# Where VectorE's spare steps stand between two seeds of a key-tile pair, in a four-layer graph network on one Trainium2 core

## The chip, the cores and the metric

The kernel runs on one core of one Trainium2 chip. Every time here is in device microseconds (us) of that core, for one launch. A core has five engines with a queue each: TensorE (PE, matrix products into PSUM banks), VectorE (DVE), ScalarE (ACT, here the exponentials), GpSimd (POOL) and SyncE (SP, which issues most DMAs). An engine takes its queue strictly in program order and waits at an instruction until the semaphores that it names are there; whatever stands behind it in that queue waits too.

## The reference

Four layers over a graph of N = 3327 nodes with 128 features, each `x = x + layer(relu(layernorm(x)), adj)`. Almost all of the time lies in the first, a graph attention with the adjacency added twice as a bias. It makes 128 heads (`d`) with 8 numbers each:

```python
q = (x @ Wq.T).reshape(d, n, h)            # d = 128 heads, n = 3327 nodes, h = 8
k = (x @ Wk.T).reshape(d, n, h)
v = (x @ Wv.T).reshape(d, n, h)
a = jnp.einsum('dnh,dmh->dnm', q, k) * scale
a = a + spatial_encoding + edge_encoding    # both are adj here
a = jax.nn.softmax(a, axis=2)
out = jnp.einsum('dnm,dmh->dnh', a, v)
return out.reshape(n, h * d) @ Wo.T
```

The other three (hyperbolic graph layers and a two-way message layer) are products with `adj` or its transpose and stand after the attention.

## The kernel before

**The attention's loops.** The scores are made transposed: key tiles of 128 rows on the partitions, queries along the free axis. The 3327 queries are cut into 7 *chunks* of 476 (index `c`), the 128 heads into 32 *groups* of four (`g`), the 26 key tiles into 13 *pairs* (`q`, 0 to 12; `r` is 0 or 1 inside the pair). So there are 7 x 32 x 13 = 2912 pairs `u`, 224 groups, and in each pair four heads `j`.

**What happens to one pair.** A pair holds two of seven PSUM banks. VectorE *seeds* each bank with adjacency minus a row bound (`seed(u, r)`, L641). TensorE adds the scores of head 0 (`scores(u, 0)`, L650), ScalarE takes the exponential of both banks at once (`exps`, L662 for 952 columns, L665 where the banks do not lie side by side and each is done alone), then TensorE adds the difference to head 1 in the same bank (the query operand holds head j minus head j-1), and so on to head 3. After the exponential of head 3 the bank is free for a later pair: `seed(m+1, 1)` and `seed(m+2, 0)` both follow the exponential of `(m-2, 3)`. The exponentials are multiplied with V into one bank `po` (`values`, L705), which VectorE copies out once a group (`store`, L713).

**The order is written out by hand.** One loop runs `i` over slots, four to a pair. In slot `i` ScalarE gets one exponential; `at = i % 4` says which of the pair's slots it is. I write `q4@0` for the slot with `at == 0` of pair 4 of a group. ScalarE's order is: `@0` head 0 of pair m, `@1` head 3 of m-2, `@2` head 2 of m-1, `@3` head 1 of m. VectorE's seeds come at `@1` (`seed(m+1, 1)`) and `@2` (`seed(m+2, 0)`). The slot in which something is written down gives its place in the queue of its engine, nothing else.

**Exponentials by hand.** In the pairs 0, 2, 5, 7 and 10 (`BY_HAND`) the exponential of head 0 of `r = 1` is made by VectorE, so that ScalarE has only one bank to do there. `hand_exp(u)` is a generator: its first step, in `@0` of the pair, is `mul` (L683, which reads the raw scores out of the bank) and the seed of that bank; then come the steps k3, k2, k1 (L687) and fin (L689, times `EA`), one for each `next()`. TensorE needs the result four pairs later. `EA` is the exponential of the bias alone, made for each chunk by `bare(c, q)`: a subtraction on VectorE (L674) and an exponential on ScalarE (L675), the second waiting for the first. For the chunks after the first, `bare` is written down eight pairs ahead, so in the pairs 5, 7, 10 and 12 of a chunk's last group and pair 2 of the next one's first.

**Squares.** The transposed adjacency and the row maxima of the chunks to come are made on the side: a `Square` of 128 rows is loaded in four quarters (`load`: four DMAs of 104 KB by SP into the only buffer `rows`), each quarter is turned in two halves (`turn`, L288, VectorE) and reduced (`largest`, L292, VectorE). Then come `gather`, `back`, `finish` and `store` (a DMA of 1664 KB). `plan` puts them under the number of a pair; in `@0` of that pair they are written down (`behind`). Three or four squares belong to a chunk, one every seven groups, 22 in the loop.

**SP's queue.** At pair 1 of each group `load_qk` and `load_v` put the next group's 40 or so loads into SP's queue; at pair 4 GpSimd is given `negate_q` (L566), `spread_v` (L576) and `all_here` for them.

Of the kernel before, what the change touches and what calls it, by code (L numbers as in the profile page):

```python
# [29 lines left out]
NQ = NT // 2  # L30
# [8 lines left out]
NG = HEADS // 4  # L39
# [25 lines left out]
def rows_of(t):  # L65
    return P - 1 if t == NT - 1 else P
# [11 lines left out]
def width_of(c):  # L78

    return min(CW, N + 1 - c * CW)  # L80


def squares_of(c):

    return 0 if c < 0 else -(-min(CW * (c + 1), NP) // P)
# [3 lines left out]
def gnn_kernel(ctx: ExitStack, tc: tile.TileContext, x, adj, Wq, Wk, Wv, Wo, embed, layer,  # L89
# [174 lines left out]
    class Square:  # L264
# [29 lines left out]
        def store(self):  # L294
            nc.sync.dma_start(by_tile[:, :, self.s * P:(self.s + 1) * P].rearrange("t p n -> p t n"), self.cols)
# [30 lines left out]
    with tc.tile_pool(name="a1", bufs=1) as a1, tc.tile_pool(name="a2", bufs=2) as a2, \  # L326
# [23 lines left out]
        for t0 in range(0, NT, 2):  # L350
            for s in "kq":
# [3 lines left out]
                for i in range(2):  # L355
                    t = t0 + i
                    sq = a4.tile([P, H, P], F32, name="sq")
# [82 lines left out]
    with tc.tile_pool(name="d1", bufs=1) as d1, tc.tile_pool(name="d2", bufs=2) as d2, \  # L440
# [17 lines left out]
        with tc.If(loose > 0):  # L458
            for s in range(squares_of(0), NT):
                square(d2, s, d2)  # L460
            for t in range(NT):
                m = rows_of(t)
# [24 lines left out]
            for c in range(NC):  # L487
# [5 lines left out]
                with tc.For_i(0, HEADS, 1) as d:  # L493
# [12 lines left out]
                    for t in range(NT):  # L506
                        m = rows_of(t)
                        s = d_ps.tile([P, 4 * P], F32, name="ps_y")
# [16 lines left out]
    with tc.tile_pool(name="e1", bufs=1) as e1, tc.tile_pool(name="e_adj", bufs=28) as e_adj, \  # L525
# [69 lines left out]
        with tc.If(loose < 1), tc.manual_schedule():  # L595
# [11 lines left out]
            pairs = [(c, g, q) for c in range(NC) for g in range(NG) for q in range(NQ)]  # L607
            n = len(pairs)
            adj_of, shift_of, v_of, e_of, here = {}, {}, {}, {}, {}
            by_vector = deque()  # L610
# [13 lines left out]
            def touch(u, rows, x):  # L624
                of = {banks(u)[r] for r in rows}
                for y, other in touched:
                    if not of & other and x.ins.engine != y.ins.engine:
                        tc.declare_no_dep(x.ins, y.ins, reason="other banks")
                for i in of:
                    if i in last:  # L630
                        tc.add_manual_dep(x.ins, last[i].ins.name, after, reason="the same bank")
                    last[i] = x
                touched.append((x, of))

            def bank(u, r):
                return S[:, banks(u)[r], :width_of(pairs[u][0])]

            def seed(u, r):
                c, g, q = pairs[u]
                w = width_of(c)  # L640
                touch(u, [r], nc.vector.tensor_tensor(bank(u, r), adj_of[c][2 * q + r][:, :w], shift_of[c][:, :w],  # L641
                                                      op=ALU.subtract))

            def scores(u, j):
                c, g, q = pairs[u]
                w, b = width_of(c), (c * NG + g) % 2
                for r in range(2):
                    hand = r == 1 and by_hand(u)
                    q_s = QZ[b] if hand and j == 1 else QS[b][:, j, :]
                    x = nc.tensor.matmul(  # L650
                        bank(u, r), KT[b][64 * r:64 * r + 64, max(0, j - 1), q * P:(q + 1) * P],
                        q_s[64 * r:64 * r + 64, :w], start=hand and j == 0, stop=True, skip_group_check=True)
                    if (j, q, r) == (0, 0, 0):
                        tc.add_manual_dep(x.ins, here.pop(c * NG + g).ins.name, after, reason="the loads")
                    touch(u, [r], x)

            def exps(u, j):
                w, (even, odd) = width_of(pairs[u][0]), banks(u)
                e = e_of[u, j] = e_e.tile([P, 2, CW], F32, name=f"e{j}", bufs=(5, 4, 3, 2)[j])
                hand = j == 0 and by_hand(u)  # L660
                if even > odd and not hand:
                    touch(u, (0, 1), nc.scalar.activation(e[:, :, :w], S[:, odd:even + 1, :w], AF.Exp, scale=2.0))  # L662
                    return
                for r in range(1 if hand else 2):
                    touch(u, [r], nc.scalar.activation(e[:, 1 - r, :w], bank(u, r), AF.Exp, scale=2.0))  # L665

            def by_hand(u):

                return 0 <= u < n and pairs[u][2] in BY_HAND

            def bare(c, q):

                w = width_of(c)
                nc.vector.tensor_tensor(EA[q][:, :w], adj_of[c][2 * q + 1][:, :w], shift_of[c][:, :w], op=ALU.subtract)  # L674
                nc.scalar.activation(EA[q][:, :w], EA[q][:, :w], AF.Exp, scale=2.0)  # L675

            def hand_exp(u):


                w = width_of(pairs[u][0])  # L680
                s = e_h.tile([P, CW], F32, name="h")[:, :w]
                e = e_of[u, 0][:, 0, :w]
                touch(u, [1], nc.vector.tensor_scalar(s, bank(u, 1), EXP_ARG, None, op0=ALU.mult))  # L683
                seed(u, 1)
                yield
                for k in (3, 2, 1):
                    nc.vector.scalar_tensor_tensor(e, s if k == 3 else e, EXP_C[k], s, op0=ALU.add, op1=ALU.mult)  # L687
                    yield
                nc.vector.scalar_tensor_tensor(e, e, EXP_C[0], EA[pairs[u][2]][:, :w], op0=ALU.add, op1=ALU.mult)  # L689
# [11 lines left out]
            def values(u, r):  # L701
                c, g, q = pairs[u]
                w, k = width_of(c), c * NG + g
                for j, (v, of) in enumerate(heads_of(u, r)):
                    nc.tensor.matmul(po[32 * j:32 * j + H + 1, :w], VA[k % 2][:, 2 * pairs[v][2] + of, j, :],  # L705
                                     e_of[v, j][:, 1 - of, :w], start=(q == 0 and r == 0),
                                     stop=(q == NQ - 1 and r == 1))
# [31 lines left out]
                        adj_of[c + 1].append(load_adj(c + 1, len(adj_of[c + 1])))  # L739


            behind = {}

            def plan(u, f, *a):
                behind.setdefault(u, []).append((f, a))

            def plan_squares(c):
                for k, s in enumerate(range(squares_of(c), squares_of(c + 1))):
                    sq, u = Square(e_t, s), (c * NG + 7 * k + 1) * NQ
                    for j in range(4):  # L750
                        plan(u, sq.load, j)
                        plan(u + 4, sq.turn, j, 0)
                        plan(u + 9, sq.turn, j, 1)
                        plan(u + 12, sq.largest, j)
                        u += NQ
                    for k, f in ((0, sq.gather), (1, sq.back), (7, sq.finish), (8, sq.store)):
                        plan(u + k, f)

# [8 lines left out]
            for c in range(NC):  # L767
                for q in BY_HAND:
                    u = c * NG * NQ + q
                    if u:  # L770
                        plan(u - 8 if c else u - 1, bare, c, q)
            bare(0, 0)

            def in_slot(i):

                j = -i % 4
                return (i - 3 * j) // 4, j


            for i in range(-4, 4 * n + 15):  # L780
                u, j = in_slot(i)
                if 0 <= u < n:
                    exps(u, j)
                at = i % 4
                if i == -4:
                    seed(0, 0)
                if at == 0 and by_hand(i // 4):
                    by_vector.append(hand_exp(i // 4))
                    next(by_vector[-1])
                for k in range(0 if at % 3 else 1 if at else 0 if by_hand(i // 4) else 2):  # L790
                    if by_vector and next(by_vector[0], True):
                        by_vector.popleft()
                if at == 0 and i > 0:
                    for f, a in behind.pop(i // 4, ()):
                        f(*a)
                if at == 1 and (i + 3) // 4 < n and not by_hand((i + 3) // 4):
                    seed((i + 3) // 4, 1)
                u = (i - 14) // 4
                if at == 2 and 0 <= u < n and pairs[u][2] == NQ - 1:
                    store(u)  # L800
                if at == 2 and (i + 6) // 4 < n:
                    seed((i + 6) // 4, 0)
                if at % 2:
                    for k in (1, 2):
                        u, j = in_slot(i + k)
                        if 0 <= u < n:
                            scores(u, j)
                    u, r = ((i - 11) // 4, 0) if at == 3 else ((i - 13) // 4, 1)
                    if 0 <= u < n:
                        values(u, r)  # L810
                if at == 0 and 0 <= i // 4 < n:
                    loads(i // 4)
# [19 lines left out]
    def arr(name, w=D):  # L832
        return big.tile([P, NT, w], F32, name=name)

    xs, ys, hT, uT = arr("xs"), (arr("y0"), arr("y1")), big.tile([P, NP], F32, name="hT"), big.tile([P, NP], F32, name="uT")
    a, w1 = arr("a", D + 1), arr("w", D + 1)
# [587 lines left out]
```

## Time and profile before

| what | value |
|---|---|
| three runs: median, lowest, highest | 11043.86, 11043.25, 11045.12 us |
| the profiled execution, its span | 11043.15 us, 11041.4 us |
| first to last exponential of the attention | 451 to 10207 us |
| ScalarE busy from 500 to 10100 us | 9533.5 of 9600 us |
| TensorE, VectorE, GpSimd busy there | 9491.1, 7872.5, 1915.4 us |
| busy before it, 0 to 451 us: TensorE, VectorE, ScalarE | 188.8, 214.2, 163.6 us |
| busy behind it, 10206 to 11041.4 us | 737.1, 478.0, 212.9 us |
| granted TensorE clock, whole run | 0.983 |

A row of the profile gives the start, the length, the engine, the line, the operation, what it writes and reads, and in brackets the idle time before it and what ended that. Records of ScalarE overlap: one that starts 0.84 us after the one before lasts 0.97 us. Its busy share therefore hides short losses, and the distance from start to start is what counts.

### The profile page before, as it was taken

The numbers are of one execution on the slowest core, as the hardware profiler recorded it, in microseconds if no ns is written. First come the engines' busy times: TensorE is split into PE (matmuls) and PEld (weight loads), VectorE is DVE, ScalarE is ACT, GpSimd is POOL, SyncE is SP. The second block draws the span as 40 slices with busy tenths as digits, with TensorE's granted clock in tenths as the row PEclk, the third lists the DMA queues.
The fourth block names the chain that finished last, engine by engine and source line by source line (L and its number), as shares of the span: only waits on it lengthen the run. The fifth ranks groups of instructions, "written<-read, shape, count | busy, mean of one in ns | idle before, by whom it ended". The sixth has DMA issues, their size and how long they took to land. (4 is left out here: it accounts for less than half of the span.)

```text
span 11041.4 us, 206142 instructions
## 1 busy us (share of the span) xinstructions
PE 10565.6 (96%) x72876; PEld 3427.7 (31%) x72876; DVE 8678.3 (79%) x13452; ACT 10058.1 (91%) x13816; POOL 2173.9 (20%) x3149
## 2 busy tenths in 40 slices
PE   4599999999999999999999999999999999999889
PEld 2133322333223322233322333222222233332544
DVE  5588887888878887788887888878887787887655
ACT  3599999999999999999999999999999999999330
POOL 5121221121211221221211211211212121211101
PEclk7799999999999999999999999999999999999899
DMA  8755555555555554555545555455545544543668
GB/s 250 253 99 92 98 97 105 98 98 91 99 110 92 98 97 82 110 98 92 99 90 112 99 96 94 91 117 92 99 86 89 109 87 80 88 83 67 199 234 282
DMA packets 697364, 1257.08 MB, mean 114 GB/s; under 512 B 195218, under 2 KB 557737, under 8 KB 683279
## 3 DMA queue, kind: packets, MB, share of 16 engines
q1 hardware_dynamic: 646060, 1114.42, 50.1%
q0 software_dynamic: 50272, 129.37, 4.1%
q8 instruction: 590, 9.67, 0.4%
q14 instruction: 442, 3.62, 0.1%
HBM read 1096.53 MB, written 146.60 MB: 113 GB/s over the span
## 5 line engine op out<-in xcount | busy, mean ns | idle before, releaser
L662 ACT ACTIVATE e<-S 128x952 f32<-128x952 f32 (+1 forms) x9024 | 8316.9, 1076 | 42.3 <-PE S L650 28.4
L705 PE MATMUL po<-e,VA 128*9 128x476 f32 (+1 forms) x46592 | 5738.7, 564 | 32.5 <-DVE OS L713 16.8
L641 DVE TENSOR_TENSOR S<-a,shb 128x476 f32<-128x476 f32 (+1 forms) x5824 | 4016.1, 690 | 1330.2 <-ACT e L662 968.4
L650 PE MATMUL S<-QS,KT 64*128 64x476 f32 (+1 forms) x22176 | 4543.4, 443 | 89.4 <-DVE S L641 29.6
L650 PEld LDWEIGHTS S<-QS,KT 64*128 64x128 f32 x22176 | 2081.6, 184 | 5096.2 <-issue 1284.8
L665 ACT ACTIVATE e<-S 128x476 f32<-128x476 f32 (+1 forms) x4128 | 2418.3, 689 | 3.7 <-PE S L650 2.9
L687 DVE SCALAR_TENSOR_TENSOR e<-e,h 128x476 f32<-128x476 f32 (+1 forms) x2240 | 1550.6, 692 | 77.1
L566 POOL TENSOR_SCALAR QS<-QS 32x476 fp32r<-32x476 f32 (+1 forms) x1344 | 1092.7, 813 | 1541.4 <-DMA QS<-qS_d 986.1
L717 POOL DMA_DIRECT2D oT_d<-OS x896 | 470.6, 530 | 4538.9 <-DVE OS L713 4494.6
L705 PEld LDWEIGHTS po<-e,VA 128*9 128x9 f32 x46592 | 691.0, 88 | 1641.1 <-issue 1522.5
L683 DVE TENSOR_SCALAR h<-S 128x476 f32<-128x476 f32 (+1 forms) x1120 | 727.8, 650 | 261.6 <-PE S L650 259.6
L689 DVE SCALAR_TENSOR_TENSOR e<-e,EA 128x476 f32<-128x476 f32 (+1 forms) x1120 | 824.0, 736 | 0.0
L687 DVE SCALAR_TENSOR_TENSOR e<-h 128x476 f32<-128x476 f32 (+1 forms) x1120 | 767.7, 685 | 0.0
L1047 PE MATMUL pu<-strip,y 128*128 128x512 f32 (+2 forms) x1456 | 600.5, 567 | 45.2 <-issue 29.2
L650 PE MATMUL S<-QZ,KT 64*128 64x476 f32 (+1 forms) x1120 | 487.6, 435 | 12.6 <-DVE S L641 8.5
L576 POOL COPY VA<-VR 128x832 f32<-128x832 f32 x224 | 247.0, 1103 | 970.8 <-DMA VR<-v_d 659.8
L1047 PEld LDWEIGHTS pu<-strip,y 128*128 128x128 f32 (+1 forms) x1456 | 273.0, 192 | 322.6 <-issue 289.3
L1051 DVE TENSOR_REDUCE deg<-strip 128x1 f32<-128x1536 f32 (+3 forms) x104 | 192.8, 1881 | 74.1 <-DMA strip<-in_adj_dram 40.8
L650 PEld LDWEIGHTS S<-QZ,KT 64*128 64x128 f32 x1120 | 205.3, 183 | 113.6 <-DVE S L641 63.9
L999 ACT COPY uT<-pu 128x512 f32<-128x512 f32 (+1 forms) x21 | 11.2, 554 | 244.3 <-PE pu L1047 244.3
L288 DVE STREAM_TRANSPOSE cols<-rows 128x416 f32<-128x416 f32 x208 | 205.2, 991 | 26.3 <-DMA rows<-in_adj_dram 18.5
L713 DVE COPY OS<-po 128x476 f32<-128x476 f32 (+1 forms) x224 | 146.3, 653 | 97.5 <-PE po L705 97.5
(242 smaller groups left out, 1973.2 us busy)
## 6 DMA issues: line engine op xcount, KB each, us to landing
KT<-kS_d SPq DMA_DIRECT2D x1792, 208.0 KB
KT<-kS_d SPq DMA_DIRECT2D x1792, 104.0 KB
VR<-v_d SPq DMA_DIRECT2D x224, 416.0 KB
QS<-qS_d SPq DMA_DIRECT2D x3072, 14.9 KB
QS<-qS_d SPq DMA_DIRECT2D x1536, 29.8 KB
adjT<-cols SPq DMA_DIRECT2D x26, 1664.0 KB
a<-adjT SPq DMA_DIRECT2D x156, 238.0 KB
rows<-in_adj_dram SPq DMA_DIRECT2D x309, 104.0 KB
```

Source lines behind the costliest of these rows:

```text
L566: nc.gpsimd.tensor_scalar(QS[b][r0:r0 + 32, j + 1, :w], QS[b][r0:r0 + 32, j, :w].bitcast(F32), -1.0, 0.0, op0=ALU.mult, op1=ALU.add)
L576: nc.gpsimd.tensor_copy(VA[(c * NG + g) % 2][:, :, :, 0:H], v.rearrange("p j (t e) -> p t j e", e=H))
L641: touch(u, [r], nc.vector.tensor_tensor(bank(u, r), adj_of[c][2 * q + r][:, :w], shift_of[c][:, :w], op=ALU.subtract))
L650: x = nc.tensor.matmul(bank(u, r), KT[b][64 * r:64 * r + 64, max(0, j - 1), q * P:(q + 1) * P], q_s[64 * r:64 * r + 64, :w], start=hand an ...
L662: touch(u, (0, 1), nc.scalar.activation(e[:, :, :w], S[:, odd:even + 1, :w], AF.Exp, scale=2.0))
L665: touch(u, [r], nc.scalar.activation(e[:, 1 - r, :w], bank(u, r), AF.Exp, scale=2.0))
L683: touch(u, [1], nc.vector.tensor_scalar(s, bank(u, 1), EXP_ARG, None, op0=ALU.mult))
L687: nc.vector.scalar_tensor_tensor(e, s if k == 3 else e, EXP_C[k], s, op0=ALU.add, op1=ALU.mult)
L689: nc.vector.scalar_tensor_tensor(e, e, EXP_C[0], EA[pairs[u][2]][:, :w], op0=ALU.add, op1=ALU.mult)
L705: nc.tensor.matmul(po[32 * j:32 * j + H + 1, :w], VA[k % 2][:, 2 * pairs[v][2] + of, j, :], e_of[v, j][:, 1 - of, :w], start=(q == 0 and r ...
L717: nc.gpsimd.dma_start(oT_d[:, d * N + c * CW:d * N + c * CW + w], o[32 * j:32 * j + H + 1, :w])
L1047: nc.tensor.matmul(got[c][:, :k], y[:m, t, :], s[:m, c * 4 * P - c0:c * 4 * P - c0 + k], start=(t == 0), stop=(t == NT - 1))
```

## The change

The polynomial steps no longer stand at `@3` (one) and `@0` (two) but together behind `seed(m+2, 0)` at `@2`: three, two where `store` stands there as well, none where the next pair is one by hand. Behind them, from a second table `between`, come the turns, the row maxima and `bare`. The square's places are counted anew: its twelve operations stand at the pairs 8 and 11 of six groups, the first quarter's load at pair 2 of the first of them, each further load one pair behind the maximum that frees the buffer; the rest follows from the seventh group on.

```diff
-            behind = {}
+            behind, between = {}, {}
 
-            def plan(u, f, *a):
-                behind.setdefault(u, []).append((f, a))
+            def plan(u, f, *a, into=behind):
+                into.setdefault(u, []).append((f, a))
 
             def plan_squares(c):
                 for k, s in enumerate(range(squares_of(c), squares_of(c + 1))):
-                    sq, u = Square(e_t, s), (c * NG + 7 * k + 1) * NQ
+                    sq, u = Square(e_t, s), (c * NG + 7 * k) * NQ
+                    at = [u + 8 + 13 * (m // 2) + 3 * (m % 2) for m in range(12)]
+                    plan(u + 2, sq.load, 0)
                     for j in range(4):
-                        plan(u, sq.load, j)
-                        plan(u + 4, sq.turn, j, 0)
-                        plan(u + 9, sq.turn, j, 1)
-                        plan(u + 12, sq.largest, j)
-                        u += NQ
+                        plan(at[3 * j], sq.turn, j, 0, into=between)
+                        plan(at[3 * j + 1], sq.turn, j, 1, into=between)
+                        plan(at[3 * j + 2], sq.largest, j, into=between)
+                        if j < 3:
+                            plan(at[3 * j + 2] + 1, sq.load, j + 1)
+                    u += 6 * NQ
                     for k, f in ((0, sq.gather), (1, sq.back), (7, sq.finish), (8, sq.store)):
                         plan(u + k, f)
...
-                        plan(u - 8 if c else u - 1, bare, c, q)
+                        plan(u - 8 if c else u - 1, bare, c, q, into=between)
...
-                for k in range(0 if at % 3 else 1 if at else 0 if by_hand(i // 4) else 2):
-                    if by_vector and next(by_vector[0], True):
-                        by_vector.popleft()
...
                 if at == 2 and (i + 6) // 4 < n:
                     seed((i + 6) // 4, 0)
+                if at == 2:
+                    stored = 0 <= u < n and pairs[u][2] == NQ - 1
+                    for k in range(0 if by_hand(i // 4 + 1) else 2 if stored else 3):
+                        if by_vector and next(by_vector[0], True):
+                            by_vector.popleft()
+                    for f, a in between.pop(i // 4, ()):
+                        f(*a)
```

## The prediction, made before the changed kernel ran

> **What bounds the kernel now.** I read the shares first, then a stretch of the attention, then single pairs in the order of time.
>
> ```profile
> PE 10565.6 (96%) x72876; PEld 3427.7 (31%) x72876; DVE 8678.3 (79%) x13452; ACT 10058.1 (91%) x13816; POOL 2173.9 (20%) x3149
> ...
> L662 ACT ACTIVATE e<-S 128x952 f32<-128x952 f32 (+1 forms) x9024 | 8316.9, 1076 | 42.3 <-PE S L650 28.4
> ...
> L689 DVE SCALAR_TENSOR_TENSOR e<-e,EA 128x476 f32<-128x476 f32 (+1 forms) x1120 | 824.0, 736 | 0.0
> ```
>
> ScalarE seems full and idle for 42 us, but its records overlap. So I took the starts of all 13,152 exponentials (9024 + 4128, in the order the loop writes) and the distance from each to the next. The tenth percentile is 0.839 us for a two-bank one and 0.444 for a single one, the medians 0.844 and 0.447. What exceeds the median of its form adds up to 294 us of the attention's 9755: that, less the work of `bare`, is all a better order can win. By place in the group: q4@0 63.9 us, q2@2 49.6, q8@0 47.3, q0@2 26.7, q9@0 15.1; the last group of a chunk carries 4.5 us instead of 1.3. Now q4@0 and q8@0, VectorE first, then ScalarE:
>
> ```profile
> 2378.80 0.65 DVE L641 TENSOR_TENSOR S<-a,shb 128x476 f32<-128x476 f32 x1
> 2379.36 0.65 DVE L687 SCALAR_TENSOR_TENSOR e<-h 128x476 f32<-128x476 f32 x1
> 2380.04 1.34 DVE L687 SCALAR_TENSOR_TENSOR e<-e,h 128x476 f32<-128x476 f32 x2
> 2381.30 1.60 DVE L641 TENSOR_TENSOR S<-a,shb 128x476 f32<-128x476 f32 x2
> ...
> 2391.64 1.03 DVE L689 SCALAR_TENSOR_TENSOR e<-e,EA 128x476 f32<-128x476 f32 x1
> 2392.59 0.64 DVE L683 TENSOR_SCALAR h<-S 128x476 f32<-128x476 f32 x1
> 2393.26 0.66 DVE L641 TENSOR_TENSOR S<-a,shb 128x476 f32<-128x476 f32 x1
> ```
>
> ```profile
> 2380.55 3.80 ACT L662 ACTIVATE e<-S 128x952 f32<-128x952 f32 x4
> ...
> 2395.82 1.02 ACT L665 ACTIVATE e<-S 128x476 f32<-128x476 f32 x2 [0.27 <-PE S L650]
> ```
>
> In pair 2 `store` runs at 2378.23, then seed(4,0), k3, k2, k1, and only at 2381.30 seed(4,1), though the exponential that frees its bank ended at 2380.3. Four exponentials at 0.84 with a last record of 0.97 need 3.49 us; they took 3.80. In pair 6 the fin of pair 5 holds the mul of pair 7 until 2392.59, the scores it reads having ended at 2391.93; seed and the next scores follow late, 0.27 us are lost. Over all groups seed(4,1) starts 0.70 us after its bank's last exponential ended, seed(9,1) 0.27, seed(8,1) and seed(12,1) 0.08, the other `r = 1` seeds 0.03 to 0.06. As 0.70 costs 0.29 (63.9/224), some 0.4 us of lateness is free.
>
> **The changes, part by part.** VectorE is in order, so only a changed order counts. Behind pairs 0, 5 and 10 it is the same three steps between the same two seeds.
>
> *Pair 2.* Now seed(4,0), fin(0), k3(2), seed(4,1). Steps that depend on each other start 0.68 apart, independent ones 0.57 (both rows above). 3 x 0.57 = 1.71 us replace the 2.50 of the rows: 0.79 earlier, more than the mean lateness. Nearly all of 63.9 goes: -63; bound -42, if TensorE (1.54 us for a half pair at its fastest, ScalarE 1.68) takes a third. k2, k1, fin(2) then stand before seed(6,0), which TensorE uses 2.9 us later.
>
> *Pair 6.* The fin of 5 moves behind seed(9,0); mul(7) starts about 0.6 earlier: -45 of 47.3. Late next is seed(9,1): released 47.3/217 = 0.22 earlier, with fin, k3, k2 before it in place of k3, k2, k1, which saves 0.11: lateness 0.27 + 0.22 - 0.11 = 0.38, at the edge. q9@0 grows: +5, bounds -10 and +30.
>
> The two-input steps lengthen where GpSimd works: fin(2) lasted 1.01 us in the 216 groups where it overlapped a GpSimd record, 0.65 in 8; fin(5) 0.86 in 56 of 224, 0.64 otherwise; mul, with one input, 0.65 either way. At pair 7 that is 56 x 0.22 = 12 us, already inside the lateness above, so nothing is added. The Trainium skill (SBUF — State Buffer, Who interferes with whom) speaks against bunching such steps: an operation with two SBUF inputs and a GpSimd one that reads SBUF lock each other out for the whole instruction. If every meeting cost the whole 0.81 us of a GpSimd record, 56 x 0.81 = 45 us would be added and the time would be some 11038; the rows show a quarter of that.
>
> *`bare`.* ScalarE's half waits in order for VectorE's half:
>
> ```profile
> 3210.01 0.65 DVE L683 TENSOR_SCALAR h<-S 128x476 f32<-128x476 f32 x1 [0.60 <-PE S L650]
> 3210.70 0.66 DVE L641 TENSOR_TENSOR S<-a,shb 128x476 f32<-128x476 f32 x1
> 3211.27 0.65 DVE L674 TENSOR_TENSOR EA<-a,shb 128x476 f32<-128x476 f32 x1
> ```
>
> ```profile
> 3210.29 0.60 ACT L665 ACTIVATE e<-S 128x476 f32<-128x476 f32 x1
> 3211.95 0.60 ACT L675 ACTIVATE EA<-EA 128x476 f32<-128x476 f32 x1 [1.06 <-DVE EA L674]
> ```
>
> Now ScalarE loses 1.05, 1.20, 0.97, 0.15 and 1.18 us at the five places (starts, as above), 4.55 a chunk. Afterwards VectorE's half stands behind the steps. Let E be the end of the exponential in @1: seed at E+0.03, the next seed +0.76, three steps +0.56, +0.69, +0.69, `bare` +0.57, its length 0.65: E+3.95. ScalarE could go on at E+0.69 (its @2 starts 0.15 before E, plus 0.84). It waits 3.3 us at pairs 5 and 10, 3.2 at 7 (two independent steps), 0.6 at 12 (no steps), 3.3 at pair 2 (`store` first: E+1.0, then 0.57 each). 13.7 - 4.55 = 9.15 us a chunk, six chunks: +55. Behind it ScalarE has everything ready, which gives back some of it: bounds +38 and +60.
>
> *Squares.* The first quarter is issued behind the same `load_qk` as before, but is wanted in the same group and not the next:
>
> ```profile
> 2782.86 0.39 SPq L571 DMA_DIRECT2D VR<-v_d  x1
> 2783.29 1.89 SPq L283 DMA_DIRECT2D rows<-in_adj_dram  x4
> ```
>
> ```profile
> 2788.47 1.42 DVE L641 TENSOR_TENSOR S<-a,shb 128x476 f32<-128x476 f32 x2
> 2789.80 0.65 DVE L689 SCALAR_TENSOR_TENSOR e<-e,EA 128x476 f32<-128x476 f32 x1
> 2791.68 0.66 DVE L641 TENSOR_TENSOR S<-a,shb 128x476 f32<-128x476 f32 x1 [1.24 <-ACT e L662]
> ```
>
> This is pair 7 to 9 of such a group. The packets ended 4.2 us after the first issue (3.7 to 5.2 elsewhere): 2787.5. The turn comes behind seed(10,0) at 2789.2, k1 and fin: 2791.0. The gap of 1.24 less a step of 0.69 leaves 0.55 for a turn of 1.00, and the mul behind seed(11,0) has 0.38 to give: covered. But the square's `store` now stands one group ahead; in the groups behind a store VR was issued at pair 6.9 to 8.5, mean 7.45, against 6.7. Three such and the very first group (9.1) are late by 0.5 to 4 us: +6, bounds 0 and +40. The later quarters follow their maximum (pair 9.4) and are wanted at 11.9, 8 us later; landing 3 us. GpSimd's memset for a quarter waits for the same maximum and has nothing due behind it until the next group. `gather`, `back` and `finish` only move a group on. The groups with turns lose 0.08 us more than the others now, 96 of them: -4. The last quarter of the last square (31 rows, landing 12 us after issue) held its group for 50.8 us, not 43.4: about half goes, -4.
>
> Sum: -63 - 45 + 5 + 55 + 6 - 8 = -50. The profiled execution took 11043.2 us, 0.7 below the median of the runs: about 10993.
>
> **The rivals.** *Late rows (slower).* If the first quarter lands behind the turn in all 22 squares, VectorE stops at pair 8 and with it the seeds. For: one buffer, in SP's queue behind a load that takes 26 us of issue, and the `store` just ahead. Against: 3 us to spare in the rows above. Each us costs 22; from 2.3 us a square the gain is gone, at 5 us the time is 11043 + 60 = 11103.
>
> *One gain given back (no change).* TensorE is 96% busy, or seed(9,1) takes over what q8@0 loses: -63 + 55 + 6 - 8 = -10, 11033; with the weaker bound for pair 2, 11054, which is slightly slower.
>
> *`bare` costs nothing more.* If ScalarE loses no more than now: 10938. Against it: the wait is in the queue's order.
>
> *The change does not do what it says.* The order on VectorE is unchanged behind three of five hand pairs; if the other two did not matter, the sum would be +55 + 6 - 8: 11096. The lateness of seed(4,1) speaks against it.
>
> **How the numbers follow.** Forecast 0.66; late rows 0.10; one gain given back 0.13; `bare` free 0.06; no effect 0.05. The forecast's own range, from the bounds, is 10955 to 11030; the whole range goes to 10950 and 11060. A measurement tells 0.2% (22 us) from no change: below 11022 is faster, 0.71; within, 0.13; slower, 0.16.
>
> **What would show it.** q4@0 and q8@0 fall from 64 and 47 us to under 10 each; seed(4,1) starts at once behind its exponential; ScalarE's waits for `EA`, 27.4 us now in the list of waits, grow to about 80; turns wait for `rows` in a few groups only. A wait of turns above 40 us, or q9@0 above 45, would make it wrong.

## The result: slower, against the forecast

| | before | changed |
|---|---|---|
| median of 4 runs (lowest, highest) | 11043.56 us (11042.22, 11045.12) | 11151.1 us (11148.95, 11158.88) |
| the profiled execution, its span | 11043.15 us, 11041.4 us | 11150.37 us, 11148.6 us |
| granted TensorE clock | 0.983 | 0.978 |

The ratio is 1.0098, 95% interval 1.0086 to 1.0109. The forecast was 10993 with a range to 11060: wrong in sign, 158 us off; the kernel is 1% slower and not 0.5% faster. The profile of the changed kernel, first the shares and the costliest group of instructions (after the bar: busy us, mean ns of one, idle before and what ended most of it):

```profile
PE 10594.4 (95%) x72876; PEld 3423.6 (31%) x72876; DVE 8791.1 (79%) x13452; ACT 10050.9 (90%) x13816; POOL 2126.1 (19%) x3149
...
L662 ACT ACTIVATE e<-S 128x952 f32<-128x952 f32 (+1 forms) x9024 | 8340.0, 1090 | 84.4 <-PE S L650 80.4
```

The shares tell nothing, as before. Before its two-bank exponentials ScalarE now stands idle for 84.4 us and not 42.3, nearly all of it for TensorE's scores. The second wait of ScalarE that grew is in the list of waits (total us, times, longest us):

```profile
ACT EA L675 <- DVE EA L674: 81.4, 30, 6.2
...
DVE cols L288 <- DMA rows<-in_adj_dram: 40.7, 13, 13.4
```

Of the 40.7 us, 13.2 lie ahead of the attention, as in the kernel before; inside it the turns wait 27.4 us, before 5.5.

**The two gains came.** The same group as in the prediction (chunk 1, group 12), pair 2 on VectorE:

```profile
2406.89 0.65 DVE L713 COPY OS<-po 128x476 f32<-128x476 f32 x1 [0.31 <-PE po L705]
2407.46 0.65 DVE L641 TENSOR_TENSOR S<-a,shb 128x476 f32<-128x476 f32 x1
2408.02 0.65 DVE L689 SCALAR_TENSOR_TENSOR e<-e,EA 128x476 f32<-128x476 f32 x1
2408.58 0.65 DVE L687 SCALAR_TENSOR_TENSOR e<-h 128x476 f32<-128x476 f32 x1
2409.15 1.42 DVE L641 TENSOR_TENSOR S<-a,shb 128x476 f32<-128x476 f32 x2
```

From the store to seed(4,1), the first of the two at 2409.15, it is 2.26 us, where it was 3.07. Over all groups seed(4,1) starts 0.05 us after its bank's last exponential ended, not 0.70; mul(7) starts 0.08 us after its scores ended, not 0.33.

**Where the time went.** For every exponential I take the distance to the one before less the median of that one's form (0.845 us for two banks, 0.447 for one), summed by place. The table has 208 ordinary groups: without the very first, the twelve on both sides of a chunk's end, and the three that hold the last square's short quarter.

| place, us in all | before | changed |
|---|---|---|
| q4@0, @1, @2 (behind pair 2) | 69.4 | -0.9 |
| q8@0 (behind pair 6) | 45.6 | 1.6 |
| q9@0 | 13.5 | 12.3 |
| q6@0 | 4.7 | 90.6 |
| q5@2, q5@3 | 0.6 | 18.7 |
| q10@2, q10@3, q11@0 | 5.3 | 23.3 |
| q0@2, q2@2 | 72.5 | 68.8 |
| all places | 211.9 | 225.4 |

So 114 us were won behind pairs 2 and 6, and 86 lost again at q6@0 alone, a place that the prediction did not have. The rest of the difference of 107.2 us in span: ordinary groups +13.5, the twelve groups at chunk ends +78.7 (there `bare` stands), the very first group +5.9, the last square's three +6.1, before and behind the attention +3.0.

**What happens at q6@0**, in chunk 1, group 14, where 0.515 us is lost. VectorE's, TensorE's, ScalarE's and GpSimd's timelines:

```profile
2497.36 1.98 DVE L687 SCALAR_TENSOR_TENSOR e<-e,h 128x476 f32<-128x476 f32 x2
2499.37 0.91 DVE L689 SCALAR_TENSOR_TENSOR e<-e,EA 128x476 f32<-128x476 f32 x1
2500.20 0.65 DVE L641 TENSOR_TENSOR S<-a,shb 128x476 f32<-128x476 f32 x1
2500.96 0.65 DVE L683 TENSOR_SCALAR h<-S 128x476 f32<-128x476 f32 x1
2501.65 2.19 DVE L641 TENSOR_TENSOR S<-a,shb 128x476 f32<-128x476 f32 x3
```

```profile
2499.64 0.94 PE L650 MATMUL S<-QS,KT 64*128 64x476 f32 x4
...
2502.36 0.48 PE L650 MATMUL S<-QZ,KT 64*128 64x476 f32 x1 [0.25 <-DVE S L641]
```

```profile
2501.99 2.00 ACT L662 ACTIVATE e<-S 128x952 f32<-128x952 f32 x2
2504.24 0.96 ACT L662 ACTIVATE e<-S 128x952 f32<-128x952 f32 x1 [0.25 <-PE S L650]
```

```profile
2496.31 3.47 POOL L566 TENSOR_SCALAR QS<-QS 32x476 fp32r<-32x476 f32 x4
```

The same pair of the same group in the kernel before, VectorE and then ScalarE:

```profile
2470.00 1.03 DVE L689 SCALAR_TENSOR_TENSOR e<-e,EA 128x476 f32<-128x476 f32 x1
2471.56 1.08 DVE L641 TENSOR_TENSOR S<-a,shb 128x476 f32<-128x476 f32 x1 [0.54 <-ACT e L662]
2472.82 0.65 DVE L683 TENSOR_SCALAR h<-S 128x476 f32<-128x476 f32 x1 [0.18 <-PE S L650]
```

```profile
2474.49 4.48 ACT L662 ACTIVATE e<-S 128x952 f32<-128x952 f32 x5
```

There only fin stands ahead of seed(6,0); VectorE waits for ScalarE before the seed and for TensorE before mul(5), and ScalarE runs on without a gap.

Read the changed kernel's rows from the back. The exponential of pair 6 at 2504.24 waits for TensorE, which is late because the scores of pair 5's bank, the product with `QZ` at 2502.36, waited 0.25 us for the seed that stands behind mul(5) (the first of three at 2501.65). mul(5) ran at 2500.96; the scores it reads were the second of those from 2499.64, and that one's record ended at 2500.13. It stood behind seed(6,0) at 2500.20, and that behind k2, k1 and fin of pair 2. These three are long: 1.98 for two and 0.91, where such steps took 1.34 for two and, in the shorter of its two rows, 0.65 in the prediction. Beside them GpSimd negates the next group's queries (2496.31 to 2499.78); that this is what stretches them is shown by `e3_no_read` below.

Means over 224 groups, in us (the last column is an experiment below):

| | before | changed | e3_no_read |
|---|---|---|---|
| k2(2), k1(2) | 0.654, 0.654 | 0.975, 0.872 | 0.648, 0.653 |
| fin(2), seed(6,0) | 0.995, 0.845 | 0.855, 0.718 | 0.653, 0.662 |
| mul(5) starts behind the end of its scores | 0.095 | 0.677 | 0.070 |

### The profile page after: what moved, and what is told of

Its sections match the earlier page's. It is cut to its first block, busy times and chain, and to the rows that moved or that the text cites. A ratio compares the mean times of both kernels' runs of the same rounds, so it can differ in the third digit from the quotient of the medians.

```text
span 11148.6 us, 205912 instructions
## 1 busy us (share of the span) xinstructions
PE 10594.4 (95%) x72876; PEld 3423.6 (31%) x72876; DVE 8791.1 (79%) x13452; ACT 10050.9 (90%) x13816; POOL 2126.1 (19%) x3149
## 5 line engine op out<-in xcount | busy, mean ns | idle before, releaser
L662 ACT ACTIVATE e<-S 128x952 f32<-128x952 f32 (+1 forms) x9024 | 8340.0, 1090 | 84.4 <-PE S L650 80.4
L665 ACT ACTIVATE e<-S 128x476 f32<-128x476 f32 (+1 forms) x4128 | 2448.6, 700 | 19.2 <-PE S L650 18.8
L687 DVE SCALAR_TENSOR_TENSOR e<-e,h 128x476 f32<-128x476 f32 (+1 forms) x2240 | 1647.5, 736 | 61.6
L566 POOL TENSOR_SCALAR QS<-QS 32x476 fp32r<-32x476 f32 (+1 forms) x1344 | 1050.4, 782 | 1512.9 <-DMA QS<-qS_d 1077.0
L288 DVE STREAM_TRANSPOSE cols<-rows 128x416 f32<-128x416 f32 x208 | 204.3, 987 | 48.7 <-DMA rows<-in_adj_dram 40.7
L1006 ACT COPY uT<-pu 128x512 f32<-128x512 f32 (+1 forms) x21 | 11.2, 554 | 244.1 <-PE pu L1054 244.1
```

The costliest lines, as they stand in the source:

```text
L566: nc.gpsimd.tensor_scalar(QS[b][r0:r0 + 32, j + 1, :w], QS[b][r0:r0 + 32, j, :w].bitcast(F32), -1.0, 0.0, op0=ALU.mult, op1=ALU.add)
```

## The experiments

Theory A: mul(5) is late because three steps, not one, stand ahead of it in pair 3 and are stretched by GpSimd's negation; `bare` is a separate loss. The rivals: the stretch does not matter; the two are one loss; the squares' new places are to blame.

**`bare` back at its old place.** `e1_bare_back`:

```diff
-                        plan(u - 8 if c else u - 1, bare, c, q, into=between)
+                        plan(u - 8 if c else u - 1, bare, c, q)
```

> The changed kernel (11151 us) with bare back at slot @0, eight pairs ahead, as before; all else as changed. Theory (bare waits behind the steps): ScalarE's waits for EA were 81.4 us in the changed kernel and 27.4 before, and the groups at a chunk's change took 78.7 us more; so 70 to 79 us come back, 11072 to 11081 us, and EA waits fall to about 27 us. Rival (the loss is all in the late seed of pair 6 and the rows): no more than 20 us come back, 11131 us or above.

Measured: 11065.44 us (11060.02 to 11073.17), ratio 1.0022 to the kernel before, 1.0013 to 1.0032. 86 us came back, a little more than expected. The groups at chunk ends fall from +78.7 to +2.0 us against before, q6@0 stays at 92.3. The wait in the list:

```profile
ACT EA L675 <- DVE EA L674: 33.4, 27, 5.3
```

So the loss at q6@0 does not hang on `bare`, and without `bare` the change is still 22 us slower than before.

**One step let into pair 1.** With fin(0) ahead of pair 2, the steps of pair 2 begin a place earlier and two are left for pair 3. `e2_early_fin`:

```diff
-                    for k in range(0 if by_hand(i // 4 + 1) else 2 if stored else 3):
+                    for k in range((i // 4 % NQ == 1) if by_hand(i // 4 + 1) else 2 if stored else 3):
```

> The changed kernel with one step allowed in pair 1, ahead of the hand pair 2: fin(0) stands there, k3 and k2 of pair 2 behind its store, and two steps instead of three (k1, fin) stand before seed(6,0) of pair 4. In the changed kernel seed(6,0) starts 0.86 us after its bank is free (0.19 before), mul(5) is queued behind it, and q6@0 and q5@3 lose 129 us together, 11 before. Theory (the third step delays mul(5) and its seed): lateness falls by 0.7 to 1.0 us, 90 to 115 us come back, 11035 to 11060 us. Rival (TensorE has no more room once q4@0 no longer waits): the loss stays, 11130 to 11155 us.

Measured: 11075.36 us (11068.0 to 11079.82), ratio 1.003 (1.0019 to 1.0042): 76 us came back, less than expected. Chunk 1, group 14 again:

```profile
2477.99 1.03 DVE L687 SCALAR_TENSOR_TENSOR e<-e,h 128x476 f32<-128x476 f32 x1
2479.05 0.91 DVE L689 SCALAR_TENSOR_TENSOR e<-e,EA 128x476 f32<-128x476 f32 x1
2479.89 1.03 DVE L641 TENSOR_TENSOR S<-a,shb 128x476 f32<-128x476 f32 x1
2481.03 0.65 DVE L683 TENSOR_SCALAR h<-S 128x476 f32<-128x476 f32 x1
```

The remaining steps are as stretched as before, and seed(6,0) with them, but there is one less: mul(5) starts 0.215 us behind the end of its scores on the mean, not 0.677, and q6@0 falls from 90.6 to 9.7 us, q5@3 from 11.2 to 1.0. ScalarE's wait for `EA` stays, 81.8 us. Not all is kept: q7@2 and q9@0 grow by 12 and 8 us, which no experiment went after.

**No negation.** GpSimd writes the same rows but reads nothing. `e3_no_read`:

```diff
-                    nc.gpsimd.tensor_scalar(QS[b][r0:r0 + 32, j + 1, :w], QS[b][r0:r0 + 32, j, :w].bitcast(F32),
-                                            -1.0, 0.0, op0=ALU.mult, op1=ALU.add)
+                    nc.gpsimd.memset(QS[b][r0:r0 + 32, j + 1, :w].bitcast(F32), 0.0)
```

> The changed kernel in which GpSimd sets the 32x476 query operands to zero instead of negating them (the negation is left out, the scores are wrong from head 1 on); so GpSimd reads no SBUF there. In the changed kernel the three steps and seed(6,0) around pair 4 last 0.92 to 1.03 us each where GpSimd negates, 0.65 elsewhere. Theory A (the stretch by GpSimd is what makes seed(6,0) late): q6@0 and q5@3 fall from 129 us to under 30, 11040 to 11060 us. Theory B (the number of steps alone): 0.69 us of extra step stays, 100 us or more stay, 11125 to 11150 us. Half each: about 11090 to 11100 us.

Measured: 11066.37 us (11058.85 to 11075.0), ratio 1.002 (1.0011 to 1.003): 85 us came back, 6 us above theory A's range. VectorE and GpSimd in the same group (its lines from 568 on stand one number lower here):

```profile
2478.02 1.33 DVE L686 SCALAR_TENSOR_TENSOR e<-e,h 128x476 f32<-128x476 f32 x2
2479.39 0.65 DVE L688 SCALAR_TENSOR_TENSOR e<-e,EA 128x476 f32<-128x476 f32 x1
2479.96 0.66 DVE L640 TENSOR_TENSOR S<-a,shb 128x476 f32<-128x476 f32 x1
2480.87 0.66 DVE L682 TENSOR_SCALAR h<-S 128x476 f32<-128x476 f32 x1 [0.25 <-PE S L649]
```

```profile
2476.90 3.21 POOL L566 MEMSET QS<- 32x476 f32 x6
```

The order on VectorE is that of the changed kernel, three steps ahead of seed(6,0), and GpSimd is at work beside them as before: its memsets, though shorter (0.49 us on the mean, the negations 0.78), overlap k2(2) in 209 of the 224 groups, the negations did in 200. But each step lasts 0.65 again, mul(5) now waits for TensorE and not the reverse, and q6@0 is -0.1 us. Without the stretch, three steps fit.

**Both of these at once.** `e2_early_fin` and `e3_no_read` together, `f3_early_fin_no_read`:

> The step in pair 1 as in e2_early_fin, and GpSimd's negation replaced by a memset of the same rows, which reads nothing (the negation is left out, so the scores of the heads behind the first are other numbers). Alone they took 76 and 85 us off. Theory A, the loss at pair 6 is one lateness with two factors: three steps ahead of seed(6,0), and their stretch where GpSimd reads; without either it is under what is free, so both together bring little more than one, 11040 to 11065. Theory B, the stretch costs by itself at other places too (pairs 5, 7 and 9): both come off separately, 11151 - 161 = 10990, between 10975 and 11010.

Measured: 11069.53 us (11065.3 to 11072.44), ratio 1.0023 (1.0014 to 1.0033). It is 6 us faster than the first alone and 3 slower than the second: place and stretch are two factors of one lateness, and taking either away brings it below what is free. The time is 5 us above the expected bound, and theory B's 10990 is far off.

**The steps alone.** The kernel before with only the new rule for the steps; squares and `bare` as they were. `e4_steps_only`:

```diff
-                for k in range(0 if at % 3 else 1 if at else 0 if by_hand(i // 4) else 2):
-                    if by_vector and next(by_vector[0], True):
-                        by_vector.popleft()
...
+                if at == 2:
+                    stored = 0 <= u < n and pairs[u][2] == NQ - 1
+                    for k in range(0 if by_hand(i // 4 + 1) else 2 if stored else 3):
+                        if by_vector and next(by_vector[0], True):
+                            by_vector.popleft()
```

> The kernel before with the new rule for the steps alone; squares and bare as before. Theory (pair 4 to 6 gives back the whole gain): q4@0 and q8@0 win 105 us, q6@0 and q5@3 lose 118, and the turn that still stands at pair 4 adds to the latter: 11050 to 11090 us. Rival (the steps' rule is a gain and bare with the squares is the whole loss): 10940 to 11000 us.

Measured: 11118.09 us (11113.8 to 11125.68), ratio 1.0073 (1.0056 to 1.0089): worse than expected, 75 us above before. All of that lies in the groups with a turn, 74 us there: the old place of the turn is pair 4, ahead of the same mul(5). VectorE and TensorE in chunk 1, group 11:

```profile
2362.69 0.99 DVE L288 STREAM_TRANSPOSE cols<-rows 128x416 f32<-128x416 f32 x1
2363.61 0.91 DVE L641 TENSOR_TENSOR S<-a,shb 128x476 f32<-128x476 f32 x1
2364.62 0.65 DVE L683 TENSOR_SCALAR h<-S 128x476 f32<-128x476 f32 x1
```

```profile
2366.03 0.48 PE L650 MATMUL S<-QZ,KT 64*128 64x476 f32 x1 [1.13 <-DVE S L641]
```

TensorE loses 1.13 us in this group, 0.25 in the one shown above, and q5@3 costs 74.5 us over the run. Since `e1_bare_back` is this kernel with the squares moved, the squares' new places are worth 11118 - 11065 = 53 us under the new steps: they take off part of the loss, and they do not cause it.

**Both repairs.** `e1_bare_back` and `e2_early_fin` together, `f1_both`:

> The change with two of its parts altered together: `bare` back at its old place behind the first exponential of a pair (as in e1_bare_back), and one step let into pair 1, so that pair 3 has two steps and not three (as in e2_early_fin). Alone they took 86 and 76 us off the 11151. Theory A, they are two separate losses (ScalarE waiting for EA; mul(5) late behind the stretched seed of pair 6): both come off, 11151 - 86 - 76 = 10989, between 10975 and 11005, and ScalarE's starts exceed their medians by about 398 - 86 - 77 = 235 us in all. Theory B, they are one loss that either removes (bare's wait only shows because the tiles around it are late, or the reverse): about 11060, as each alone. What it shows of the forecast: with A, squares and steps as forecast would have given some 10990 without the two terms that were mis-sized.

Measured: 10993.32 us (10989.28 to 10999.67), ratio 0.9958 (0.9941 to 0.9975). The two losses add up as two: 11151 - 86 - 76 = 10989. The excess over the medians is 241 us in all, 235 expected.

**`bare` cut in two.** VectorE's half goes where the steps leave room, ScalarE's half a pair later. `f2_split`, on top of `e2_early_fin`:

```diff
+            def bare_exp(c, q):
+                w = width_of(c)
                 nc.scalar.activation(EA[q][:, :w], EA[q][:, :w], AF.Exp, scale=2.0)
...
-                        plan(u - 8 if c else u - 1, bare, c, q, into=between)
+                        v = c * NG * NQ + {0: -5, 2: -2, 5: -2, 7: 3, 10: 6}[q] if c else u - 1
+                        plan(v, bare, c, q, into=between)
+                        plan(v + {5: 2}.get(q, 1) if c else v, bare_exp, c, q, into=between)
```

> The change with the step in pair 1, and `bare` cut in two: VectorE's half stands where the steps leave room (pairs 8 and twice 11 of a chunk's last group, pairs 3 and 6 of the next chunk's first), ScalarE's half one pair later (two for EA5), when it has nothing to wait for. Theory A, the price of `bare` is ScalarE waiting in the order of its queue for VectorE's half: the wait of L675 for EA L674, 27 us in before and 81 in the change, falls to under 5, and the time is that of f1_both less the 27 us that before still paid: about 10962, between 10950 and 10975. Theory B, the 0.65 us of VectorE's half itself delays the next seed wherever it stands: 30 places lose 0.5 us or more each behind it, and the time is no better than f1_both (10985 to 11010).

Measured: 10968.07 us (10964.58 to 10970.65), ratio 0.9933 (0.9916 to 0.9949), 25 us under `f1_both`. One of VectorE's halves with the seed behind it, and its exponential on ScalarE (L678 here):

```profile
3210.94 0.65 DVE L674 TENSOR_TENSOR EA<-a,shb 128x476 f32<-128x476 f32 x1
...
3211.79 0.66 DVE L641 TENSOR_TENSOR S<-a,shb 128x476 f32<-128x476 f32 x1 [0.21 <-ACT e L662]
```

```profile
3208.07 4.54 ACT L662 ACTIVATE e<-S 128x952 f32<-128x952 f32 x5
3212.29 0.81 ACT L678 ACTIVATE EA<-EA 128x476 f32<-128x476 f32 x1
```

The next seed still waits for ScalarE, so VectorE's half costs nothing there, and ScalarE stays without a gap. The twelve groups are 27.4 us shorter than in the kernel before. The wait for `EA` came down to 10.0 us, not under 5.

**The squares a group later**, with the first quarter eleven pairs ahead of its turn. `f4_split_rows`, on top of `f2_split`:

```diff
-                    at = [u + 8 + 13 * (m // 2) + 3 * (m % 2) for m in range(12)]
-                    plan(u + 2, sq.load, 0)
+                    at = [u + 21 + 13 * (m // 2) + 3 * (m % 2) for m in range(12)]
+                    plan(u + 10, sq.load, 0)
...
-                    u += 6 * NQ
+                    u += 7 * NQ
```

> f2_split with the squares one group later and their first quarter fetched eleven pairs ahead of its turn and not six. Theory A (the forecast's own term): rows that land late cost some 6 us in four groups, and a store ahead of them does the rest: 5 to 15 us faster than f2_split, and the turns' wait for rows falls from about 40 us to under 25. Theory B: the rows' lateness is covered, within 4 us of f2_split.

Measured: 10958.07 us (10957.35 to 10961.15), ratio 0.9925 (0.9908 to 0.9941), the fastest of all: 85 us under the kernel before. 10 us under `f2_split`, 6.8 of them in the very first group. The turns' wait came down to 26.9 us, not under 25; the longest stays:

```profile
DVE cols L288 <- DMA rows<-in_adj_dram: 26.9, 7, 12.9
```

Of these, 14.0 us lie ahead of the attention; inside it only the longest is left (22.8 us in five waits in `f2_split`). It belongs to the last square's quarter of 31 rows. Against the kernel before, the group that holds this wait is 13 us longer in the changed kernel and 14 here: no experiment touched it.

## Why the prediction was wrong

- *Pair 2, -63.* Right: -70 us with the two places behind it, and seed(4,1) is no longer late.
- *Pair 6, -45, and q9@0, +5.* Right: -44 and -1.
- ***The step that failed.*** "k2, k1, fin(2) then stand before seed(6,0), which TensorE uses 2.9 us later." That looked at the user of the seed and not at the instruction behind it in VectorE's queue. Behind seed(6,0) stands mul(5), and behind that the seed of the same bank, which TensorE uses at once (0.06 us later). The term was priced at nothing and measured +86 us at q6@0. Another 18 us came at q5@2 and q5@3. It took two things, and the runs of before showed the ground of both: two more steps ahead of mul(5), which started only 0.10 us behind its scores then, and steps that lengthen beside GpSimd, as fin(2) did with 1.01 us. The prediction had priced the second only for pair 7. Without either one (`e2_early_fin`, `e3_no_read`) q6@0 falls to 10 us or to none.
- *The rule on GpSimd.* The Trainium skill (SBUF — State Buffer, Who interferes with whom) says that a two-input operation contends with a GpSimd instruction that reads SBUF and not with one that only writes. `e3_no_read` agrees: beside the memsets the steps keep their 0.65 us. A lock for the whole instruction, as the prediction quotes it, does not show; the amount here is less than a whole record of 0.78: 0.37 us for k2(2) by its median, 0.26 for k1(2) and fin(2). The prediction said that nothing is to be added for it. At pair 7 that held; in pair 3 it is what decides, 85 us.
- *`bare`, +55.* The wait in the queue was read rightly, but the term is short: +78.7 us in the twelve groups. The wait for `EA` is 81.4 us, forecast 80, and at the five places ScalarE loses 12.9 us a chunk (13.7 forecast, 5.1 in before), which is 47 us in six chunks. The other 32 us are lost in the pairs behind the places, 5.3 a chunk. So "Behind it ScalarE has everything ready, which gives back some of it" is the part that failed, and the trace shows what came in its place: TensorE runs at half its clock there. ScalarE at one chunk's first place, then TensorE, then a stretch of 3.40 us with TensorE's busy time (3.40, 20 products) and the granted clock (0.50):

```profile
3242.44 1.94 ACT L662 ACTIVATE e<-S 128x952 f32<-128x952 f32 x2
3247.88 0.60 ACT L675 ACTIVATE EA<-EA 128x476 f32<-128x476 f32 x1 [3.50 <-DVE EA L674]
...
3255.21 1.03 ACT L665 ACTIVATE e<-S 128x476 f32<-128x476 f32 x2 [1.02 <-PE S L650]
```

```profile
3249.38 1.39 PE L650 MATMUL S<-QS,KT 64*128 64x476 f32 x4 [2.76 <-ACT e L662]
...
3252.71 1.77 PE L705 MATMUL po<-e,VA 128*9 128x476 f32 x8
...
3255.32 0.98 PE L705 MATMUL po<-e,VA 128*9 128x476 f32 x8
```

```profile
3251.60:3255.00 3.40, 3.40 (x20) 0.50 0.40 92
```

ScalarE's stop leaves TensorE idle for 2.76 us; then eight value products last 1.77 us and not 0.98, and ScalarE waits 1.02 us for scores. The same stands at 23 of the 30 places: TensorE idle for 2.1 to 3.3 us, then 3.4 or 6.8 us at a granted clock of 0.50, and behind it 1.0 or 1.9 us lost on the mean. At the other seven TensorE was idle for 1.4 us at most and the clock stayed; at the one of these with a long wait for `EA`, 2.4 us, nothing is lost behind it. `f1_both` and `f2_split`, without the long stops, have no such stretch at these places. No run changed the clock alone.

- *Late rows, +6, and the squares, -8.* Late rows cost the first group +5.9 us and nothing much elsewhere (`f4_split_rows`, with the rows fetched earlier, takes it back); the last square's quarter moved its loss to the next group and grew by 6 us instead of shrinking by 4.
- *The range.* With every bound at its best the sum gives the 10955 of the range; with every bound at its worst it gives 11078, not 11030. The measured time lies above that too.
- *The rivals.* None was right. "Late rows" had the sign, with the wrong cause: inside the attention turns waited 27.4 us for rows, one of them alone 13.4. "One gain given back" had a gain taken over by a later place, but at q9@0, which stayed at 12 us. Of the signs named beforehand, the wait of turns passed its 40 us only with the 13.2 us ahead of the attention.
- *A match by chance.* With both losses repaired (`f1_both`) the kernel takes 10993 us, the very number of the forecast. That does not bear the sum out. `bare` costs no more than before there (-3.4 us in the twelve groups), so the forecast's other terms alone would give 10938, and 55 us are missing. Against before, 46 us more are lost in the 208 ordinary groups at q5@2, q5@3, q6@0, q7@2, q9@0 and around q10 and q11, places where the sum had 5 us in all; why, no run shows.

## What to carry to other kernels

When a step is moved ahead of an instruction on an in-order engine, follow the queue past that instruction to the first one whose result is used at once, and price the wait there; the user of the next instruction alone says nothing. Size the room for steps from their length beside the other engines' work in that place, not from the shortest rows. When one helper issues work on two engines, the second waits in its queue for the first: write the two halves down apart, with enough other work between them that the first half is done. And price a stop also by what stands behind it: here a stop of 2 us or more on TensorE was mostly followed by several us at half its clock.

## What the runs showed that was not expected

Two remedies for one loss do not add: GpSimd's reads stretch four instructions of pair 3 by 0.80 us a group in the changed kernel (the sum of the table's four means, 3.42, less the last column's 2.62), and yet with one step fewer in the way the reads cost 6 us at most (11075 us with them, 11070 without). And a stop of ScalarE cost more than its own length: the five places of `bare` took 47 us more than before, the pairs behind them, with TensorE at half its clock, another 32. From 500 to 10050 us there are 26 such stretches in the changed kernel (137 us in all, before 7), 23 in each of the other runs with `bare` behind the steps, and one to three in every other run; this is also why the granted clock of the whole run is 0.978 and not 0.983.
